# Seven block products for four in the first layer of the second FFN, with sums of weights made in the first FFN

## The chip, the cores and the metric

One core of a Trainium2 chip runs the whole program. The time is the device time of one execution in microseconds, and the kernel before ran three times: 799.74, 795.3 and 798.07, with a median of 798.07. The engines are TensorE (PE in the profile; its weight loads are PEld), VectorE (DVE), ScalarE (ACT), GpSimd (POOL) and SyncE (SP), which issues transfers only. All times below are in microseconds unless they are marked otherwise.

## The reference

The program is one "macaron" block over 8192 rows (8 x 1024) of H = 256 numbers in float32:

```python
x = x + 0.5 * ffn(x)          # first FFN   (x0 -> x1)
x = x + memory_layer(x)       # recurrent memory layer (x1 -> x2)
x = x + 0.5 * ffn(x)          # second FFN, the same weights (x2 -> out)

def ffn(x):                   # mixture of E = 8 experts, each row goes to its best one
    h = layernorm(x)
    p = softmax(h @ gate_w);  e = argmax(p)         # top 1
    # per expert the first CAP = 320 of its rows, in the order of the 8192
    y = relu(h[rows of e] @ w1[e]) @ w2[e]          # w1: 256 x 1024, w2: 1024 x 256
    return p[e] * y                                 # rows over the capacity get zero
```

The listing is a summary in the kernel's own terms. The layer norm's division is moved behind the ReLU: the kernel only subtracts the mean in front of the first layer, and the row's 1/std is part of the factor called `gate`.

## The kernel before

`macaron` (L1307) runs three stages one after the other: the first FFN (`first_router`, then `experts` with the name f1), `attention`, and the second FFN (`experts` with f2). x1 and x2 lie in DRAM. The router of the first FFN leaves the rows it has read in four SBUF tiles with the tag xt, and `copied` writes them to x1, so that rows which no expert takes stay as they are.

`experts` (L271) has a loop over the eight experts. Each expert takes 320 rows in three blocks of 128, 128 and 64 ("slots" s = 0, 1, 2). For expert e:

- `gather` (L284) brings the rows into xg by three indirect transfers on GpSimd's queue, two experts ahead; `gate_of` (L295) brings the factors into gate by three more.
- `center` (L306) subtracts each row's mean: statistics (L311), their aggregate (L312) and the subtraction (L313), all on VectorE.
- `turn` (L317) transposes the 320 rows on TensorE (L323) and copies the result to xT (L327, ScalarE). For expert 0 alone, `turn_one` (L330) does this block by block, and the first layer's matmuls begin with the first 128 rows.
- First layer: for each of the eight f (128 of the 1024 hidden features) two matmuls of 128 x 128 weights by 320 columns (L384), then a ReLU from PSUM to hT on ScalarE (L391).
- `turn` for expert e+1 follows, and then the second layer. First the last 64 rows are done, as two halves of 64 x 128 (16 matmuls, L414). VectorE multiplies by the gate and adds the row (L424) into xh, and xh is scattered to the result (L427). Then come the 128 rows of s = 0 and of s = 1 (8 matmuls each, L441), with VectorE's L448 into xo and a scatter (L451) for each.

The order of the instructions on each engine is the order in which the program writes them (`manual_schedule`). Each engine takes its own queue strictly in that order. GpSimd's queue holds, for an expert: two scatters of the expert before, three gates, the scatter of xh, three gathers, and so on. All scatters of a stage write the same DRAM tensor, and each waits until the one before it has landed.

The searches for which rows an expert takes (`Slots.begin`, `counts`, `tokens`) serve two experts at a time. A table `searches` puts them between the first layer's matmuls of experts 0, 1 and 2. They use TensorE for counting matmuls, ScalarE for a copy and VectorE for comparisons and sums.

`Weights.load` (L263) brings w1 and w2 of an expert, 1 MB each, on SP's queue; there are two buffers of each. The PSUM pool has the banks t (three), h (three) and y (two): t for the transposes, h for the first layer, y for the second.

The attention stage waits for the first FFN. Its first loads of x1 (L690, on ScalarE's queue) come behind all scatters. The list `ORDER` sets the order within that stage; it isn't changed. Its prologue prepares wg from w_g, b_g and norm_g (L601 to L605).

Of the kernel before, what the change touches and what calls it, by code (L numbers as in the profile page):

```python
# [10 lines left out]
F32 = mybir.dt.float32  # L11
# [7 lines left out]
P = 128  # L19
# [7 lines left out]
NS = 3  # L27
# [121 lines left out]
class Slots:  # L149
# [10 lines left out]
    def __init__(self, sh, pool, pp, dr, routed):  # L160
        self.sh, self.pool, self.pp, self.dr, self.routed = sh, pool, pp, dr, routed
# [25 lines left out]
    def spread(self, _):  # L187

        nc = self.sh.nc
        t_ps = self.pp.tile([P, 512], F32, tag="t", name="t_ps")  # L190
# [6 lines left out]
    def begin(self, q, between=lambda n: None):  # L197

        nc, sh, pool, pp = self.sh.nc, self.sh, self.pool, self.pp

        d_ps = pp.tile([P, 512], F32, tag="y", name="d_ps", bufs=2)
# [5 lines left out]
        between(1)  # L207
        b_ps = pp.tile([P, 512], F32, tag="h", name="b_ps")
        nc.tensor.matmul(b_ps[:, 0:1], lhsT=sh.before, rhs=dg[:, P - 1 : P], start=True, stop=True)
        between(1)  # L210
        began = pool.tile([P, NS * P], F32, tag="began", name="began", bufs=2)
        nc.vector.tensor_scalar(began, sh.jrow, b_ps[:, 0:1], None, ALU.is_ge)
        self.began = began

    def counts(self, q, tag="y"):
# [4 lines left out]
            self.pp.tile([P, 512], F32, tag=tag, name="r_ps", bufs={"y": 2, "h": 3}[tag])[  # L220
                :, : NS * (P + 1)
            ].rearrange("p (s r) -> p s r", s=NS)
# [34 lines left out]
class Weights:  # L257


    def __init__(self, nc, pool, w1, w2):  # L260
        self.nc, self.pool, self.w1, self.w2, self.at = nc, pool, w1, w2, {}

    def load(self, e):  # L263
        a = self.pool.tile([P, 2, F], F32, tag="w1", name="w1t")
        self.nc.sync.dma_start(a, self.w1[e].rearrange("(c p) f -> p c f", p=P))
        b = self.pool.tile([P, FC, H], F32, tag="w2", name="w2t")
        self.nc.sync.dma_start(b, self.w2[e].rearrange("(c p) d -> p c d", p=P))
        self.at[e] = a, b


def experts(sh, routed, src, dst, weights, dr, name, idle=0):  # L271
# [4 lines left out]
    nc, tc = sh.nc, sh.tc  # L276
    with ExitStack() as st:
        rp = st.enter_context(tc.tile_pool(name=f"{name}_r", bufs=1))
        ep = st.enter_context(tc.tile_pool(name=f"{name}_e", bufs=2))
        pp = st.enter_context(tc.tile_pool(name=f"{name}_p", bufs=3, space=PSUM))  # L280
        slots = Slots(sh, rp, pp, dr, routed)
# [24 lines left out]
        def center(xg):  # L306

            ln = ep.tile([P, NS, 8], F32, tag="ln", name="ln")
            xn = ep.tile([P, NS, H], F32, tag="xn", name="xn")
            for s in range(NS):  # L310
                nc.vector.bn_stats(ln[:, s, :6], xg[:, s, :])  # L311
                nc.vector.bn_aggr(ln[:, s, 6:], ln[:, s, :6])  # L312
                nc.vector.tensor_scalar(xn[:, s, :], xg[:, s, :], ln[:, s, 6:7], None, ALU.subtract)  # L313
            return xn

        def turn(xn):

            xT = ep.tile([P, 2, CAP], F32, tag="xT", name="xT")
            pts = [pp.tile([P, 512], F32, tag="t", name="pt") for _ in range(2)]
            for s in range(NS):  # L320
                m = min(P, CAP - s * P)
                for c in range(2):
                    nc.tensor.transpose(  # L323
                        pts[c][:, s * P : s * P + m], xn[:m, s, c * P : (c + 1) * P], sh.ident[:m, :m]
                    )
            for c in range(2):
                nc.scalar.copy(xT[:, c, :], pts[c][:, :CAP])  # L327
            return xT

        def turn_one(xn, xT, s):  # L330

            m = min(P, CAP - s * P)
            pt = pp.tile([P, 512], F32, tag="t", name="pt")
# [6 lines left out]
        def keep(n):  # L340

            if n:
                sh.idle(pp.tile([P, 512], F32, tag="y", name="idle", bufs=2), n)

        st.enter_context(tc.manual_schedule(engines=sh.engines))
        keep(idle)
        slots.begin(0, keep)
        slots.exps()
# [1029 lines left out]
```

## Time and profile before

| what | value |
|---|---|
| median of three runs | 798.07 |
| the profiled execution itself | 801.52 |
| its span in the profile | 799.7 |
| busy PE / VectorE / ScalarE / GpSimd | 731.1 / 454.4 / 348.0 / 473.6 |
| mean clock granted to TensorE | 0.968 |
| L384, first layer: matmuls, both FFNs | 147.3 in 576 records |
| L441, second layer: matmuls, both FFNs | 114.8 in 512 records |
| a steady expert slot of the first FFN (118.87 to 137.19) | 18.32 |
| from expert 1's slot to the last scatter (82.06 to 210.71) | 128.65 |
| first load of x1 in attention | 213.86 |
| start of the second FFN's first gate transfers | 638.85 |

The busy times are those of one execution, taken by the hardware profiler. A float32 matmul runs as two passes, and each pass is a record of its own, so one matmul of the program is two records. The records of neighbouring passes overlap[...]; the distance between the starts of two records is the price of a pass. A line of a timeline gives start, length, engine, line, operation, what it writes and reads, and in brackets the idle time before it and what released it.

### The profile page before, as it was taken

How to read it: one execution, taken by the hardware profiler on the slowest of the kernel's cores; microseconds unless marked ns; L12 is line 12 of the kernel's file. 1: busy time of each engine (PE TensorE's matmuls, PEld its weight loads, DVE VectorE, ACT ScalarE, POOL GpSimd, SP SyncE). 2: the span in 40 equal slices, each digit the busy share in tenths (PEclk: the TensorE clock that was granted, in tenths of full speed). 3: DMA queues.
4: the chain of work that ended last, by engine and by line, in shares of the span. 5: the costliest groups of instructions: out<-in, count | busy, mean ns of one | idle time of the engine just before them, and what ended most of it. 6: DMA issues, size and time to landing. Idle time of an engine off the chain costs nothing. (4 is left out here: it accounts for less than half of the span.)

```text
span 799.7 us, 13992 instructions
## 1 busy us (share of the span) xinstructions
PE 731.1 (91%) x5368; PEld 541.7 (68%) x5368; DVE 454.4 (57%) x941; ACT 348.0 (44%) x756; POOL 473.6 (59%) x606
## 2 busy tenths in 40 slices
PE   7988999999668999899999999999968789999997
PEld 5667777777425486666757576675755577778775
DVE  7772343220328978988887878888763624322310
ACT  5521222222057576767666666766443222222221
POOL 6643444552134788988888888886864434455431
PEclk9998999999968999999999989999999999999999
DMA  9995445540214242454454343444405814444510
GB/s 297 368 385 168 151 147 157 174 156 17 94 54 81 82 106 82 104 169 99 159 135 132 111 103 118 96 132 108 133 28 196 293 57 142 142 150 153 153 66 23
DMA packets 110946, 110.41 MB, mean 138 GB/s; under 512 B 12384, under 2 KB 103904, under 8 KB 110880
## 3 DMA queue, kind: packets, MB, share of 16 engines
q1 hardware_dynamic: 73152, 66.43, 28.0%
q10 hardware_dynamic: 31840, 31.53, 12.5%
q0 software_dynamic: 5888, 11.57, 4.7%
q8 instruction: 42, 0.69, 0.4%
q14 instruction: 24, 0.20, 0.1%
HBM read 78.80 MB, written 30.64 MB: 137 GB/s over the span
## 5 line engine op out<-in xcount | busy, mean ns | idle before, releaser
L391 ACT ACTIVATE hT<-ph 128x320 f32<-128x320 f32 (+2 forms) x144 | 58.3, 407 | 222.4 <-PE ph L384 196.4
L384 PE MATMUL ph<-xT,w1t 128*128 128x320 f32 (+2 forms) x576 | 147.3, 411 | 2.9 <-ACT hT L391 1.9
L384 PEld LDWEIGHTS ph<-xT,w1t 128*128 128x128 f32 x576 | 104.5, 194 | 37.7 <-ACT hT L391 2.2
L441 PE MATMUL py<-w2t,hT 128*128 128x256 f32 x512 | 114.8, 382 | 0.0
L441 PEld LDWEIGHTS py<-w2t,hT 128*128 128x128 f32 x512 | 96.0, 190 | 15.1 <-issue 2.7
L424 DVE SCALAR_TENSOR_TENSOR xh<-py,gate,xg 64x128 f32<-64x128 f32 x32 | 11.2, 350 | 111.5 <-PE py L414 111.2
L448 DVE SCALAR_TENSOR_TENSOR xo<-py,gate,xg 128x256 f32<-128x256 f32 x32 | 15.5, 484 | 94.3 <-PE py L441 59.2
L806 PE MATMUL pre<-xT,w 128*64 128x512 f32 x256 | 61.4, 603 | 0.8 <-ACT kk L838 0.8
L1142 PE MATMUL pre<-wg,xT 128*128 128x256 f32 x256 | 59.1, 390 | 2.0 <-DVE m L901 2.0
L298 POOL DMA_INDIRECT gate<-gate_d,get x48 | 46.0, 959 | 21.6 <-issue 13.4
L1142 PEld LDWEIGHTS pre<-wg,xT 128*128 128x128 f32 x256 | 49.0, 194 | 10.0 <-DVE m L901 2.4
L1186 POOL TENSOR_TENSOR xo<-xo,xr 128x512 f32<-128x512 f32 x32 | 42.9, 1354 | 17.4 <-DVE xo L1180 17.4
L708 ACT ACTIVATE xt<-xt,ln_nm,lx_t 128x256 f32<-128x256 f32 x64 | 34.4, 592 | 24.2 <-POOL ln_nm L703 24.2
L1180 DVE SCALAR_TENSOR_TENSOR xo<-tail,rs,gate 128x256 f32<-128x256 f32 x64 | 27.1, 475 | 23.7 <-DMA out<-xo 12.0
L427 POOL DMA_INDIRECT x<-xh,put x8 | 8.1, 1009 | 54.3 <-DVE xh L424 44.0
L995 DVE TENSOR_TENSOR gc<-ehd,c 128x1536 f32<-128x1536 f32 x16 | 40.0, 2539 | 0.3
L427 POOL DMA_INDIRECT out<-xh,put x8 | 8.1, 1013 | 52.5 <-DVE xh L424 52.5
L806 PEld LDWEIGHTS pre<-xT,w 128*64 128x64 f32 x256 | 15.8, 136 | 30.3 <-issue 22.4
L907 POOL TENSOR_TENSOR abq<-qq,ab 128x512 f32<-128x512 f32 x16 | 33.7, 2108 | 0.9 <-DMA ab<-kept 0.9
L715 PE MATMUL pre<-ident,xt 128*128 128x128 f32 x128 | 21.0, 298 | 14.3 <-ACT xt L708 12.9
L451 POOL DMA_INDIRECT out<-xo,put x16 | 16.1, 1006 | 27.5 <-DVE xn L313 14.2
L414 PE MATMUL py<-w2t,hT 128*64 128x128 f32 x512 | 32.2, 280 | 0.0
(259 smaller groups left out, 1612.5 us busy)
## 6 DMA issues: line engine op xcount, KB each, us to landing
w1t<-w_in SPq DMA_DIRECT2D x16, 1024.0 KB
w2t<-w_in SPq DMA_DIRECT2D x16, 1024.0 KB
xt<-hidden_in SPq DMA_DIRECT2D x16, 512.0 KB
x<-xt SPq DMA_DIRECT2D x16, 512.0 KB
xt<-x ACTq DMA_DIRECT2D x16, 512.0 KB
xr<-x ACTq DMA_DIRECT2D x16, 512.0 KB
x<-xo ACTq DMA_DIRECT2D x14, 512.0 KB
out<-xo ACTq DMA_DIRECT2D x14, 512.0 KB
```

The costliest lines, as they stand in the source:

```text
L298: nc.gpsimd.indirect_dma_start(out=gate[:, s : s + 1], out_offset=None, in_=slots.gate, in_offset=bass.IndirectOffsetOnAxis(ap=slots.get[: ...
L384: nc.tensor.matmul(ph[:, at_slots], lhsT=a[:, c, f * P : (f + 1) * P], rhs=at[:, c, at_slots], start=(c == 0), stop=(c == 1),)
L391: nc.scalar.activation(hT[:, f, at_slots], ph[:, at_slots], AF.Relu)
L414: nc.tensor.matmul(py[h * D : (h + 1) * D, :P], lhsT=hT[:, f, 2 * P :], rhs=b[:, f, h * P : (h + 1) * P], start=(f == 0), stop=(f == FC - ...
L441: nc.tensor.matmul(py[:, :H], lhsT=hT[:, f, s * P : (s + 1) * P], rhs=b[:, f, :], start=(f == 0), stop=(f == FC - 1),)
L708: self.nc.scalar.activation(x, x, AF.Identity, bias=u.nm[:, j : j + 1], scale=u.r16[:, j : j + 1])
L806: self.nc.tensor.matmul(ps[self.half[r], :], lhsT=self.w3[:, k, f * D : (f + 1) * D], rhs=u.xT[:, k].rearrange("h (p r t) -> h p r t", p=N ...
L907: self.nc.gpsimd.tensor_tensor(u.abq[:, n], u.kv[2], u.ab[:, n], ALU.mult)
L995: self.nc.vector.tensor_tensor(u.gc[:, layer], g.unsqueeze(2).to_broadcast([P, B, 3, D]), u.c3.rearrange("s n j -> s j n").unsqueeze(3).to ...
L1142: self.nc.tensor.matmul(ps[:, q * H : (q + 1) * H], lhsT=u.xT[:, k, j * P : (j + 1) * P], rhs=self.wg[:, k, :], start=(k == 0), stop=(k == 1),
L1180: self.nc.vector.scalar_tensor_tensor(u.xo[h][:, j, :], self.out_of(u, h, j), u.rs[h][:, j : j + 1], u.gate[n][:, j % 2, :], ALU.mult, ALU ...
L1186: self.nc.gpsimd.tensor_tensor(u.xo[h][:, two], u.xo[h][:, two], u.xr[h][:, two], ALU.add)
```

## The change

In the second FFN, from expert 1 on, the first layer is computed in another form. The 256 x 1024 weights are seen as four groups g of 256 x 256, each of them 2 x 2 blocks of 128 x 128, and xT as 2 x 2 blocks of 128 x 160. A product of 2 x 2 blocks is done with seven block products (Winograd's form) rather than eight. So a group has 7 matmuls of 128 x 128 weights by 160 columns, where it had 4 of 320 columns; the whole layer has 28 in place of 16. It needs four sums of weight blocks (s), four sums of blocks of xT (t, made by three VectorE operations in `row_sums`), and sums of the products, made by one ScalarE copy and VectorE operations on the way from PSUM to hT (`one` to `five`).

The sums of weights are 128 x 2048 numbers per expert. In the first FFN GpSimd makes them for experts 1 to 7 by four `tensor_tensor` operations of 128 x 512, and writes each expert's 1 MB to DRAM by a transfer on its own queue (`keep`). Both stand behind the gates of that expert. The second FFN loads them on SP's queue. In the first FFN the sums lie in the four buffers of the tag xt.

The further edits are these. The centered rows are negated: ScalarE computes mean minus row, the matmuls yield the negative, and ReLU has the scale -1. `center` for expert e+2 is issued in expert e's second layer, behind L424. `gate_of(e)` is issued at the start of expert e, where it was in expert e-1 at f = 1. `gather` runs three experts ahead. The searches stand in the second layer of experts 1 to 3; those of expert 0 stay in its first layer, with expert 2's gather and expert 1's `center` behind them at f = 1. The last 64 rows' second layer takes f = 6 last. PSUM has tags x, z, t and y, two banks each. In attention's prologue wg is computed by two operations of full size where it had two of full size and one small one.

```diff
+    def sums(self, e):
+        s = self.s[e] = self.place().rearrange("p a b -> p (a b)")[:, : 2 * F].rearrange(
+            "p (n g m) -> p n g m", n=4, m=P
+        )
+        if e in self.kept:
+            self.nc.sync.dma_start(s, self.kept[e])
+            return
+        (a11, a12), (a21, a22) = self.a[e]
+        for n, (x, y, op) in enumerate(
+            (
+                (a21, a22, ALU.add),
+                (s[:, 0], a11, ALU.subtract),
+                (a11, a21, ALU.subtract),
+                (a12, s[:, 1], ALU.subtract),
+            )
+        ):
+            self.nc.gpsimd.tensor_tensor(s[:, n], x, y, op)
+
+    def keep(self, e):
+        self.kept[e] = self.dr.tile([P, 4, FC // 2, P], F32, name=f"sums{e}")
+        self.nc.gpsimd.dma_start(self.kept[e], self.s[e])
...
         def center(xg):
-                nc.vector.tensor_scalar(xn[:, s, :], xg[:, s, :], ln[:, s, 6:7], None, ALU.subtract)
+                nc.scalar.activation(xn[:, s, :], xg[:, s, :], AF.Identity, bias=ln[:, 6:7], scale=-1.0)
...
+        def row_sums(xT):
+            nc.vector.tensor_tensor(t[:, 0:2], v[:, 1:4:2], v[:, 0:2], ALU.subtract)
+            nc.vector.tensor_tensor(t[:, 2], v[:, 3], t[:, 0], ALU.subtract)
+            nc.vector.tensor_tensor(t[:, 3], v[:, 2], t[:, 2], ALU.subtract)
...
             for f in range(FC):
                 hidden(f, slice(P if e == 0 else 0, CAP))
-                for search, n in searches.get((e, f), ()):
-                    search(n)
-                if f == 1 and e + 1 < E:
-                    gates.append(gate_of(e + 1))
+                if (e, f) == (0, 1):
+                    slots.counts(1)
+                    slots.tokens(2)
+                    rows.append(gather(2))
+                    xns[1] = center(rows[1])
+                if (e, f) == (0, 3):
+                    slots.tokens(3)
+                if (e, f) == (0, 5):
+                    slots.begin(2)
+                if (e, f) == (0, 6):
+                    slots.began_at()
...
+            def one(self, g):
+                x = self.x[g] = bank("x", "x")
+                self.product(x[:, :HC], self.s[:, 1], g, self.t[:, 2])
+                self.product(x[:, HC : 2 * HC], self.a[0][0], g, self.b[:, 0, 0], stop=False)
+                p6 = ep.tile([P, HC], F32, tag="p6", name="p6")
+                nc.scalar.copy(p6, x[:, :HC])
+                u = self.u[g] = ep.tile([P, HC], F32, tag="u", name="u", bufs=3)
+                nc.vector.tensor_tensor(u, x[:, HC : 2 * HC], p6, ALU.add)
+            def two(self, g):
+                z = self.z[g] = bank("z", "z")
+                self.product(z[:, :HC], self.s[:, 2], g, self.t[:, 1])
+                self.product(z[:, HC : 2 * HC], self.a[1][1], g, self.t[:, 3])
+                self.product(z[:, 2 * HC : 3 * HC], self.s[:, 0], g, self.t[:, 0], stop=False)
+                v = self.v[g] = ep.tile([P, 1, HC], F32, tag="v", name="v")
+                nc.vector.tensor_tensor(v[:, 0], z[:, :HC], self.u[g], ALU.add)
+            def three(self, g):
+                nc.vector.tensor_tensor(
+                    self.hT[:, 2 * g + 1, :].rearrange("p (j n) -> p j n", j=2),
+                    self.z[g][:, HC : 3 * HC].rearrange("p (j n) -> p j n", j=2),
+                    self.v[g].to_broadcast([P, 2, HC]),
+                    ALU.add,
+                )
+            def four(self, g):
+                x = self.x[g]
+                self.product(x[:, HC : 2 * HC], self.a[0][1], g, self.b[:, 1, 0], start=False)
+                nc.scalar.activation(self.hT[:, 2 * g, :HC], x[:, HC : 2 * HC], AF.Relu, scale=-1.0)
+            def five(self, g):
+                z = self.z[g]
+                self.product(z[:, 2 * HC : 3 * HC], self.s[:, 3], g, self.b[:, 1, 1], start=False)
+                nc.vector.tensor_tensor(self.hT[:, 2 * g, HC:], z[:, 2 * HC : 3 * HC], self.u[g], ALU.add)
+            def relu(self, f, a=0):
+                h = self.hT[:, f, a:]
+                nc.scalar.activation(h, h, AF.Relu, scale=-1.0)
...
+        searches = {
+            (1, 0): lambda: slots.counts(2),
+            (1, 1): lambda: slots.tokens(4),
+            (1, 2): lambda: slots.tokens(5),
+            (2, 0): lambda: slots.begin(3),
+            (2, 2): slots.began_at,
+            (3, 0): lambda: slots.counts(3),
+            (3, 1): lambda: slots.tokens(6),
+            (3, 2): lambda: slots.tokens(7),
+        }
         for e in range(E):
+            if 0 < e < E - 1:
+                if seven:
+                    weights.sums(e + 1)
+                weights.first(e + 1)
+                weights.second(e + 1)
+            if e > 0:
+                gates.append(gate_of(e))
+            if e > 0 and not seven:
+                weights.sums(e)
+                weights.keep(e)
+            if not seven or e == 0:
+                hT = plain(e, xn, xT)
+            else:
+                first = First(e, xT, t)
+                for g in range(G):
+                    first.one(g)
+                    if g > 0:
+                        first.four(g - 1)
+                    first.two(g)
+                    if g > 0:
+                        first.five(g - 1)
+                    first.three(g)
+                    if g > 0:
+                        first.relu(2 * g - 1)
+                        first.relu(2 * g - 2, HC)
+                first.four(G - 1)
+                first.relu(2 * G - 1)
             if e + 1 < E:
                 turn(xn[e + 1], xT)
+            if seven and e > 0:
+                first.five(G - 1)
+                first.relu(2 * G - 2, HC)
+            if seven and e + 1 < E:
+                t = row_sums(xT)
...
+            search(e, 0)
             for h in range(2):
                 part = slice(h * D, (h + 1) * D)
                 nc.vector.scalar_tensor_tensor(
                     xh[part], py[part, :P], gate[part, 2:3], xg[part, 2, h * P : (h + 1) * P], ALU.mult, ALU.add
                 )
+            if e + 2 < E:
+                xn[e + 2] = center(rows[e + 2])
+            search(e, 1)
             nc.gpsimd.indirect_dma_start(
...
-            if e + 2 < E:
-                rows.append(gather(e + 2))
+            if e + 3 < E:
+                rows.append(gather(e + 3))
             for s in range(2):
...
+                if s == 0:
+                    search(e, 2)
                 nc.gpsimd.indirect_dma_start(
```

## The prediction

> **What bounds the kernel now.** I read the engine totals first, then stretches of the trace, then GpSimd's timeline. "Expert slot" is the time in which TensorE works on one expert; S is its start.
>
> ```profile
> PE 731.1 (91%) x5368; PEld 541.7 (68%) x5368; DVE 454.4 (57%) x941; ACT 348.0 (44%) x756; POOL 473.6 (59%) x606
> ...
> 118.87:137.19 18.32, 18.32 (x103) 14.50 (x102) 4.43 (x13) 4.25 (x10) 8.77 (x10) 1.00 0.51 155
> 82.06:210.71 128.65, 127.11 (x718) 100.25 (x717) 33.04 (x99) 28.39 (x67) 51.82 (x53) 1.00 0.39 122
> ```
>
> The windows' columns are length, then busy time of PE, PE's weight loads, VectorE, ScalarE and GpSimd, then PE's clock, DMA share and GB/s. In a steady expert slot PE is busy for all 18.32 us; GpSimd shows 8.77. So PE sets FFN1's length, and a gain of PE in FFN2 counts in full. But GpSimd's busy time is not what its queue costs. Its timeline (start, length, what; in brackets the idle time before it and who ended it):
>
> ```profile
> 118.06 1.01 POOL L451 DMA_INDIRECT x<-xo,put  x1 [0.30 <-issue]
> 121.42 1.00 POOL L451 DMA_INDIRECT x<-xo,put  x1 [2.35 <-DVE ln L312]
> 122.72 0.98 POOL L298 DMA_INDIRECT gate<-gate_d,get  x1 [0.30 <-issue]
> ...
> 131.29 1.01 POOL L427 DMA_INDIRECT x<-xh,put  x1 [5.07 <-DVE xh L424]
> ...
> 207.26 0.98 POOL L451 DMA_INDIRECT x<-xo,put  x1 [2.43 <-DVE xo L448]
> 210.71 0.98 POOL L451 DMA_INDIRECT x<-xo,put  x1 [2.47 <-DVE xo L448]
> ```
>
> Each indirect transfer takes 1.0 and 0.3 follows before the next. Two scatters to x1 in a row stand 3.4 apart (118.06 to 121.42, 207.26 to 210.71): the second waits until the first has landed, since VectorE, named there, was done long before. In one slot this leaves 5.07 of true waiting for PE's result. That is all the room that GpSimd's queue has.
>
> **The change, 1: PE in FFN2.** Half-passes (every fp32 matmul is two) in fully busy stretches:
>
> ```profile
> 640.70:641.48 0.78, 0.78 (x8) 0.78 (x8) 0.43 (x2) 0.40 (x2) 0.48 (x2) 1.00 0.00 0
> 641.48:642.78 1.30, 1.30 (x10) 1.18 (x8) 0.00 (x0) 0.31 (x2) 0.99 (x2) 1.00 0.02 0
> 703.22:711.56 8.34, 8.34 (x32) 5.84 (x31) 3.25 (x10) 3.06 (x7) 3.89 (x4) 1.00 0.50 159
> ```
>
> These are 128, 192 and 320 moving columns, with other weights for each. Seven spacings in 0.78 are 0.112 (one record overlaps from before), eight in 1.30 are 0.1625, 31 in 8.34 are 0.269. Between 128 and 192 columns, 160 are an estimated 0.137. An expert's first layer goes from 16x2x0.269 = 8.61 to 28x2x0.137 = 7.67, so -0.94 for each of experts 1 to 7: -6.6.
>
> A rule speaks against it. The Trainium skill, "TensorE: Matmul & The Clock Gate", Part 3 (packing), has a weight load overlap a running matmul only where the row groups differ, and gives some 107 ns for 128 columns. Here all rows are used: 56x(0.133+0.107) = 13.4 per expert, +4.8 instead of -0.94, over seven +34. The rows decide: 0.112 at 128 columns holds no separate load. I take -6.6.
>
> What the block form adds beside PE: per group of two f's one ScalarE copy and three ReLUs (some 1.4 by L391's 0.28 to 0.41), and four VectorE sums (about 1.65 by L448's 0.48 and L424's 0.35), against 1.92 of PE. They hide; if a link is 0.5 later than PE can look ahead, it costs up to that in each of 28 groups (+14). The last product of a layer needs the last VectorE sum: six transposes (0.8) cover it in experts 1 to 6, for which I add 0.1 each, in expert 7 nothing does: +0.7. Searches leave the first layer: expert 1 takes 20.67 now, 2 takes 19.38; placed in the second layer I get 19.3, 19.2 and, for expert 3, 19.3 against 18.3: -0.4 together on PE's old base. The 1 MB more of loads on SP's queue per expert makes 3.7 MB in 17.4, or 215 GB/s, under the 385 of the page's early slices: nothing; without that cover 1 MB is 2.7. FFN2: -6.6+0.6+0.7-0.4 = -5.7.
>
> **2: GpSimd in FFN1.** Four sums and one 1 MB write per expert 1 to 7 now stand behind the gates and ahead of the scatter of xh, the gathers, and both scatters of xo, on the same queue. Price of one sum of 128x512:
>
> ```profile
> L1014 POOL TENSOR_TENSOR go<-go 128x512 f32<-128x512 f32 x7 | 9.1, 1294 | 0.6
> L907 POOL TENSOR_TENSOR abq<-qq,ab 128x512 f32<-128x512 f32 x16 | 33.7, 2108 | 0.9 <-DMA ab<-kept 0.9
> ```
>
> L1014 adds two strided halves, as the sums do: 1.29, and 0.06 to the next is 1.35. L907, beside a busy VectorE, takes 2.1. The skill's "GPSIMD Engine Reference", section 3.1, has some 2.6 cycles an element for two inputs, with 4497 ns for 2048; a quarter of that is an estimated 1.12, 28x0.23 = 6.4 less over the stage. The row decides, as it is this chip at this shape. The write (`keep`) has no row: nearest is an indirect transfer of 128 rows, 1.0+0.3; ends 0.4 (as ScalarE's queue pays at L195) and 2. I take 1.3.
>
> Period: gates 3x1.28 = 3.8, sums 5.4, keep 1.3, xh 1.3, gathers 3.8, first xo to second 3.4, to the next gate 1.3: 20.3, above PE's 18.3. So GpSimd sets FFN1's rate. Who waits: the gates of later experts come behind, so VectorE's line L424 (its place before the changed one), then the py bank, then PE, by a microsecond or two; no separate cost, since GpSimd stays last. Experts 1 to 4: 4x20.3, and 0.45 for expert 1's gather waiting for tokens(4): 81.7. Experts 5 and 6 have no gather; then the second scatter waits for xh's landing, 3.4, or 4.2 if behind the 1 MB: 3.8+5.4+1.3+3.8+3.4+1.3 = 19.0 each, 38.0. Expert 7 to its last scatter: the same without the last 1.3, 17.7. Sum 137.4 against 128.65 (82.06, first gate behind expert 0's scatters, to 210.71): +8.7. The attention stage waits 1:1 on that last scatter at 210.71:
>
> ```profile
> 213.59 0.52 POOL L631 MEMSET st<- 128x512 f32 x1 [1.90 <-PE pre L596]
> 213.86 1.52 ACTq L690 DMA_DIRECT2D xt<-x  x3
> ```
>
> The load of x1 is issued 2.15 after the last scatter's end. Bounds of the block: with sums of 1.05 (GpSimd's multiplications at L1010 take 1.06) and keep at 0.4, -14.7 of queue, of which PE's pace keeps all under 18.3: about +0.8. With sums of 2.1: 28x0.75 = +21 more.
>
> The subtraction in `center` goes from VectorE to ScalarE, both with room in steady slots: nothing (exposed 3x0.59, the mean of L708, per expert). The prologue's two lines for wg are hidden until x1 is loaded: nothing; exposed under 1.
>
> **3: expert 0, both FFNs.** Three Identity operations now stand in ScalarE's queue ahead of the first xT copy, and wait for the gather's third block:
>
> ```profile
> 50.30 0.37 ACT L336 COPY xT<-pt 128x256 f32<-128x256 f32 x1 [1.89 <-PE pt L335]
> ...
> 51.69 0.43 DVE L311 BATCH_NORM_STATS2 ln<-xg 128x6 f32<-128x256 f32 x1 [0.87 <-DMA xg<-hidden_in,get]
> ```
>
> The third statistics end at 52.3, and one Identity of 0.59 after 0.18 more leaves the copy at 53.1: +2.8 in FFN1, and by the same reckoning +1.8 in FFN2. Later, ScalarE's ReLU of f=1 stands behind center(1)'s Identities, which follow VectorE's tokens(2) (1.85 of small operations) and three statistics (0.61 each): 1.85+1.83+0.59 = 4.3, less some 2.4 for PE's two free banks and the count's matmuls: +1.9; and the new wait for `began` at f=6 +0.65. What may go away is this stretch as it is now:
>
> ```profile
> 59.00:63.27 4.27, 1.77 (x12) 1.43 (x10) 2.15 (x9) 0.66 (x3) 2.33 (x3) 1.00 0.86 290
> 63.27:70.10 6.83, 6.07 (x30) 5.53 (x32) 0.42 (x1) 2.12 (x7) 0.00 (x0) 0.50 0.22 58
> ```
>
> PE idles 3.3 (its b_ps comes late), then runs at half clock, losing 3.4; in FFN2 the like is 1.9 and 1.7. If both go, FFN1 changes by 2.8+2.55-3.3-3.4 = -1.35 and FFN2 by 1.8+2.55-1.9-1.7 = +0.75; if the half clock stays, +2.05 and +2.45; if the idling stays too, +5.35 and +4.35. An idle PE precedes the half clock here, and PE will idle for the 1.9 again, so I take values near the middle: +1.0 and +1.5.
>
> **Sum.** 8.7+1.0-5.7+1.5 = +5.5, on the profiled execution's 801.52 (span 799.7). The three runs had a median of 798.07, 3.45 less; the difference is carried over: 803.5.
>
> **Rivals.**
> A. GpSimd's cover holds (the other side). Place: its queue in FFN1; it decides where sums and keep fit in 18.3-13.6 = 4.7 a slot, for example sums at 0.95 and keep at 0.9. Then FFN1 gains only the tail, about +0.8, and with +0.8-5.7+2.5 it is 795.7; with expert 0 warm (-0.6 for 2.5) 792.6. For it: multiplications at 1.06, the skill's 1.12. Against: every addition at 128x512 takes 1.27 or more.
> B. GpSimd is slowed by VectorE, sums at 1.7 to 2.1: 28x0.35 to 0.75, so +10 to +21 more: 813 to 825. For it: L907; against: VectorE is 24% busy in the slot.
> C. The change doesn't do what it says on PE: ScalarE's or VectorE's chain bounds the first layer, and FFN2 gains nothing: 809. For it: 0.3 to 0.5 of room a group. With loads not overlapped, 840.
> D. The main case, but expert 0 at half clock and idle in both: 5.35+4.35 for 2.5, so 810.7.
>
> **How the numbers follow.** Main case with its own spread (799 to 811, D in it) 0.58; A 0.21, B 0.12, C 0.09. The range to 794 cuts off the lower half of A, to 815 most of B's. 0.5% is 4 us, about what a measurement of this kernel can tell from no change. Faster (under 794.1): half of A and a little, 0.13. Same (to 802.1): the rest of A and 0.15 of the main case, 0.26. Slower 0.61.
>
> **What would show it.** FFN1: GpSimd without true waiting in experts 1 to 4, slots of 20.3, PE idle in the later ones; x1 load about 10 later. FFN2: slots of 17.4 and half-passes at 0.137. The sums at 1.3 and keep at 1.3. It is wrong if the four sums end within 4.7 less keep, if the chain of `one` to `three` leaves gaps on PE, or if expert 0 goes the other way.

## The result and the profile after

The changed kernel takes 840.62 us (median of 4 runs, 837.91 to 846.82), the kernel before 798.78 (4 runs). The ratio is 1.0563, with a 95% interval of 1.0518 to 1.0609: slower by about 42 us. The prediction said 803.5, with a range from 794 to 815. The direction was right and the size was not.

The two profiled executions have spans of 799.7 and 840.8. The rows "first FFN" and "second FFN" of this table run between the issues of GpSimd's transfers, so they can be read off its timeline; "e0" is expert 0.

| stage | before | after | difference | predicted |
|---|---|---|---|---|
| to the second scatter of xo of e0, first FFN | 80.80 | 80.70 | -0.1 | +1.0 |
| first FFN, from there to its last scatter | 129.91 | 158.83 | +28.9 | +8.7 |
| attention: from there to the second FFN's first gather | 417.82 | 425.53 | +7.7 | 0 |
| second FFN, first gather to e0's second scatter of xo | 36.97 | 35.59 | -1.4 | +1.5 |
| second FFN, from there to its last scatter | 129.29 | 134.67 | +5.4 | -5.7 |
| behind the last scatter | 4.9 | 5.5 | +0.6 | 0 |

The engine totals and stretches that answer to those of before, from the page and from the windows view (length, busy time of PE, PE's weight loads, VectorE, ScalarE and GpSimd, PE's clock, DMA share, GB/s):

```profile
PE 740.4 (88%) x5536; PEld 562.7 (67%) x5536; DVE 483.1 (57%) x1025; ACT 378.7 (45%) x860; POOL 513.4 (61%) x641
```

```profile
82.01:239.53 157.52, 135.01 (x730) 104.60 (x729) 30.32 (x89) 35.49 (x81) 91.20 (x88) 0.95 0.42 142
...
736.94:744.28 7.34, 7.34 (x56) 7.34 (x55) 4.93 (x15) 3.41 (x12) 2.18 (x3) 1.00 0.64 203
744.41:765.30 20.89, 18.14 (x135) 16.02 (x134) 12.50 (x40) 6.75 (x21) 8.80 (x9) 1.00 0.57 186
```

PE is busy 9.3 longer than before and GpSimd 39.8. The first row of the windows is the first FFN from the first gate behind expert 0: 157.5 where it was 128.65, and PE now idles for 22 of it. TensorE's clock is 0.95 there, but that isn't what makes it longer. The scatter of xh, which needs TensorE's result, never waits on GpSimd's queue for more than the 0.3 that follow any instruction. Before, it waited 44.0 in all for VectorE's xh (GpSimd's waits over 80.7 to 210.8, with the total, the number of times and the longest):

```profile
POOL x L427 <- DVE xh L424: 44.0, 7, 9.8
```

The second row is the first layer of one expert of the second FFN in its new form. The 53 spacings of its 54 recorded half-passes are 0.135 to 0.137, so weight loads do not add to them. The third row is a slot of the second FFN: 20.89 long, of which PE is idle for 2.7.

Now GpSimd's timeline in the first FFN, one slot of the changed kernel from its gates to its second scatter of xo:

```profile
108.79 0.94 POOL L337 DMA_INDIRECT gate<-gate_d,get  x1 [0.30 <-issue]
109.76 1.29 POOL L293 TENSOR_TENSOR s<-w1t 128x512 f32<-128x512 f32 x1
...
113.58 1.28 POOL L293 TENSOR_TENSOR s<-w1t,s 128x512 f32<-128x512 f32 x1
115.15 0.60 POOL L297 DMA_DIRECT2D sums<-s  x1 [0.30 <-POOL s L293]
116.06 1.03 POOL L587 DMA_INDIRECT x<-xh,put  x1 [0.30 <-issue]
117.39 1.00 POOL L326 DMA_INDIRECT xg<-hidden_in,get  x1 [0.30 <-issue]
...
125.03 1.01 POOL L613 DMA_INDIRECT x<-xo,put  x1 [4.13 <-issue]
130.40 0.99 POOL L613 DMA_INDIRECT x<-xo,put  x1 [4.36 <-issue]
```

The four sums take 5.4 from 109.76 to the write at 115.15, as predicted. The write itself takes 0.9 of the queue, less than predicted. But the first scatter of xo goes out 9.0 behind that of xh, and the second 5.4 behind the first, where two scatters stood 3.4 apart before. These are waits for landings, 4.13 and 4.36, and the prediction had counted none for the first and some 2 for the second. The page's DMA list and SyncE's timeline of this slot show what travels at that time:

```profile
sums<-s POOLq DMA_DIRECT2D x7, 1024.0 KB, 8.7
```

```profile
114.88 0.37 SPq L266 DMA_DIRECT2D w1t<-w_in  x1
115.90 0.37 SPq L274 DMA_DIRECT2D w2t<-w_in  x1
```

w1's next load waits for a buffer that the sums read. It goes out when they end (114.88), w2's load stands behind it on SyncE's queue and follows (115.90), and the write comes between (115.15): 3 MB are issued in one microsecond, just ahead of the scatter of xh at 116.06. In the slots of experts 3 to 5 w1's load goes out 0.3 ahead of the write too, and w2's 2.3 to 2.9 behind it. The write needs 8.7 to land (median of seven).

The run holds a comparison of its own. Experts 5 and 6 both have sums and a write, and neither has a gather; but behind expert 5's sums the last loads of w1 and w2 go out (188.12 and 190.72), and behind expert 6's none does. From the scatter of xh to the first of xo it is 8.66 with the loads and 4.37 without:

```profile
189.28 1.02 POOL L587 DMA_INDIRECT x<-xh,put  x1 [0.30 <-issue]
197.94 0.99 POOL L613 DMA_INDIRECT x<-xo,put  x1 [7.63 <-issue]
...
212.20 1.02 POOL L587 DMA_INDIRECT x<-xh,put  x1 [0.30 <-issue]
216.57 0.99 POOL L613 DMA_INDIRECT x<-xo,put  x1 [3.36 <-DMA x<-xh,put]
```

VectorE had the rows for both ready (L608 ends at 187.5 and 208.5).

In the second FFN, VectorE's waits say which input of the first multiply by the gate (L424 before, L581 after) came last. The view's columns are the total, the number of times and the longest; before, over 660 to 770:

```profile
DVE xh L424 <- PE py L414: 40.4, 6, 7.7
```

After, over 690 to 810, and one of these in VectorE's timeline:

```profile
DVE xh L581 <- DMA gate<-gate_d,get: 22.7, 4, 5.8
```

```profile
732.61 0.71 DVE L581 SCALAR_TENSOR_TENSOR xh<-py,gate,xg 64x128 f32<-64x128 f32 x2 [5.82 <-DMA gate<-gate_d,get]
```

Before, it waited for PE. Now it waits for the gate, which GpSimd issued from 724.92 to 727.57, and TensorE waits for the bank that this multiply frees (its waits over 690 to 840):

```profile
PE py L601 <- DVE xh L581: 9.1, 4, 2.7
```

From expert 0's second scatter of xo to the last, PE is busy 128.1 of 129.3 before and 123.2 of 134.7 after. So the block products save what they should, and 10 of new idle time outweigh it.

### The profile page after: what moved, and what is told of

It reads as the page before. It is cut to its first block, busy times and chain, and to the rows that moved or that the text cites. A ratio compares the mean times of both kernels' runs of the same rounds, so it can differ in the third digit from the quotient of the medians.

```text
span 840.8 us, 14684 instructions
## 1 busy us (share of the span) xinstructions
PE 740.4 (88%) x5536; PEld 562.7 (67%) x5536; DVE 483.1 (57%) x1025; ACT 378.7 (45%) x860; POOL 513.4 (61%) x641
## 5 line engine op out<-in xcount | busy, mean ns | idle before, releaser
L601 PE MATMUL py<-w2t,hT 128*128 128x256 f32 x512 | 123.0, 397 | 26.0 <-DVE xh L581 26.0
L601 PEld LDWEIGHTS py<-w2t,hT 128*128 128x128 f32 x512 | 99.1, 198 | 45.3 <-DVE xh L581 29.6
L581 DVE SCALAR_TENSOR_TENSOR xh<-py,gate,xg 64x128 f32<-64x128 f32 x32 | 11.2, 350 | 140.0 <-DMA gate<-gate_d,get 124.3
L394 PE MATMUL ph<-xT,w1t 128*128 128x320 f32 (+2 forms) x352 | 83.4, 393 | 5.5 <-ACT xT L383 3.0
L394 PEld LDWEIGHTS ph<-xT,w1t 128*128 128x128 f32 x352 | 61.7, 196 | 23.7 <-ACT xT L383 3.5
L401 ACT ACTIVATE hT<-ph 128x320 f32<-128x320 f32 (+2 forms) x88 | 33.5, 388 | 79.4 <-PE ph L394 79.3
L352 ACT ACTIVATE xn<-xg,ln 128x256 f32<-128x256 f32 x48 | 24.3, 508 | 86.3 <-DVE ln L351 47.4
L1347 POOL TENSOR_TENSOR xo<-xo,xr 128x512 f32<-128x512 f32 x32 | 42.9, 1353 | 18.4 <-DVE xo L1341 18.3
L613 POOL DMA_INDIRECT x<-xo,put x16 | 16.0, 1000 | 53.9 <-issue 32.3
L608 DVE SCALAR_TENSOR_TENSOR xo<-py,gate,xg 128x256 f32<-128x256 f32 x32 | 15.5, 483 | 38.1 <-PE py L601 37.7
L326 POOL DMA_INDIRECT xg<-x,get x24 | 23.0, 960 | 19.1 <-issue 11.0
```

The costliest lines, as they stand in the source:

```text
L394: nc.tensor.matmul(ph[:, at_slots], lhsT=weights.w[e][:, c, f * P : (f + 1) * P], rhs=xT[:, c, at_slots], start=(c == 0), stop=(c == 1),)
L401: nc.scalar.activation(hT[:, f, at_slots], ph[:, at_slots], AF.Relu, scale=-1.0)
L601: nc.tensor.matmul(py[:, :H], lhsT=hT[:, f, s * P : (s + 1) * P], rhs=b[:, f, :], start=(f == 0), stop=(f == FC - 1),)
L613: nc.gpsimd.indirect_dma_start(out=dst, out_offset=bass.IndirectOffsetOnAxis(ap=slots.put[:, e, s : s + 1], axis=0), in_=xo[:, s, :], in_o ...
L1347: self.nc.gpsimd.tensor_tensor(u.xo[h][:, two], u.xo[h][:, two], u.xr[h][:, two], ALU.add)
```

## The experiments

"Stretch" is the second row of the first table, the first FFN from expert 0's second scatter of xo to the last scatter.

**Sums and write, each alone.** a1_no_write drops the write in `keep` (and loads w1 in place of the sums in the second FFN); a2_no_sums drops the additions and writes w1's tile; a3_write_on_sync changes the queue. Here and below, "..." stands for lines left out.

```diff
 a1:  -        self.nc.gpsimd.dma_start(self.kept[e], self.s[e])
      +        self.kept[e] = True
 ...
 a2:  -        for n, (x, y, op) in enumerate(
      +        for n, (x, y, op) in (lambda v: ())(
 ...
      -        self.nc.gpsimd.dma_start(self.kept[e], self.s[e])
      +        self.nc.gpsimd.dma_start(self.kept[e].rearrange("p n g m -> p (n g m)"), self.w[e].rearrange("p c f -> p (c f)"))
 a3:  -        self.nc.gpsimd.dma_start(self.kept[e], self.s[e])
      +        self.nc.sync.dma_start(self.kept[e], self.s[e])
```

> GpSimd makes the sums as in the changed kernel, but the 1 MB write per expert is left out; the second FFN loads the same number of bytes from w1 instead (so its first layers use wrong numbers). Measure: the first FFN from its first gate behind expert 0 to its last scatter, 128.7 us in the kernel before and 157.5 us in the changed one. Theory W (the write's packets, ahead of the scatters' in the same queue, hold up the landings on which the next scatter waits): experts 1 to 4 take 19.0 us, 5 and 6 fall back to 18.3, in all 130 to 133 us, so about 815 us of time. Theory Q (only the queue's instructions count, the write with 0.9): 157.5 less 7 x 0.9, 151 us, about 834 us.

> The four sums per expert are left out in the first FFN and the write takes w1's tile instead, 1 MB as well (the second FFN's first layers use wrong numbers). Theory W: the write still stands ahead of the scatters, but 5.4 us more lie between it and the scatter of xh, so most of it has landed: 130 to 137 us for the stretch. Theory Q: 157.5 less 7 x 5.4 is under TensorE's pace, so 129 us. A third theory, that the added traffic alone slows the loads and scatters: over 145 us.

> The write of the sums is issued on SyncE's queue, which carries the weight loads, in place of GpSimd's; all else as in the changed kernel. Theory W: the scatters have their queue for themselves, slots of about 19.2 us for experts 1 to 4 and 18.3 after, 131 to 135 us for the stretch, some 817 us of time. Theory Q: 157.5 less 7 x 0.9, 151 us. The theory of traffic as such: no better than 150 us, since the bytes and their time are the same.

| kernel | stretch | above before |
|---|---|---|
| before | 129.9 | |
| changed | 158.8 | +28.9 |
| a1, sums without the write | 137.8 | +7.9 |
| a2, write without the sums | 130.8 | +0.9 |
| a3, write on SyncE's queue | 149.6 | +19.7 |

The texts above count from the first gate, 1.3 later than this table; by their measure a1 has 136.5, a2 129.5 and a3 148.2. The sums alone cost 7.9, the write alone 0.9, and both 28.9. Part of this is slack: a little more work on GpSimd's queue hides where the queue waited for TensorE before. But the prediction had that slack in its sum and came to only 8.7 for both; the rest is in their meeting. a2 takes the meeting away as well as the sums. Its write reads w1's tile, so w1's next load waits for the write to land (SyncE's waits over 84 to 220):

```profile
SPq L266 <- DMA sums<-w1t: 66.2, 5, 17.4
```

So 0.9 is the price of a write that no load of w1 runs beside, not of a write as such. a2's 129.5 also lies as near to theory Q's 129 as to W's 130. Theory Q is out by a1 (151 expected). a1 ends somewhat over W's range; its w1 and w2 loads still go out together beside the scatter of xh (135.26 and 136.10, with the scatter at 135.4). a3 is a miss for W as it stood: with the scatters' queue free of the write, 19.7 of the 28.9 stay, close to what the theory of traffic as such expected. So it is not only that packets stand behind the write in one queue. In a3 the first scatter of xo still waits 3.88 for the landing of xh, and the second 3.68:

```profile
111.95 1.01 POOL L587 DMA_INDIRECT x<-xh,put  x1 [0.16 <-issue]
...
120.61 1.00 POOL L613 DMA_INDIRECT x<-xo,put  x1 [3.88 <-DMA x<-xh,put]
125.29 0.99 POOL L613 DMA_INDIRECT x<-xo,put  x1 [3.68 <-issue]
```

As whole executions, one each, the three took 818.2, 818.2 and 834.7, beside one of 808.1 of the kernel before. a2's stretch is 7.0 shorter than a1's, but its attention is 3.7 and its second FFN 2.9 longer. In the profiles with an unchanged second FFN (changed, a3, c1, c3, c4) this stage runs from 170.3 to 178.8 from the first gather to the last scatter; in the two longest (a3, c3) more than 10 of it are at half clock, in the changed kernel 3.4. So one such length is not good to better than some 8, and the stretches, not the whole times, carry the argument.

**When the 3 MB meet.** The next theory (B in the texts below) was that the sums release the loads at the wrong moment. c1_three_w1 was to take that away by a third buffer for w1. c3_write_later leaves the sums and moves the write to the next expert, on the same queue. c4_sums_ahead in addition makes the sums one expert ahead, so that they are not the last readers of the buffer that the next load needs.

```diff
 c1:  +        self.nw = 3 if place else 2
 ...
      -        a = self.pool.tile([P, 2, F], F32, tag="w1", name="w1t")
      +        a = self.pool.tile([P, 2, F], F32, tag="w1", name="w1t", bufs=self.nw)
 c3:  -                weights.sums(e)
      -                weights.keep(e)
      +            if e > 1 and not seven:
      +                weights.keep(e - 1)
      +            if e > 0 and not seven:
      +                weights.sums(e)
      +                if e == E - 1:
      +                    weights.keep(e)
 c4:  -                weights.sums(e)
 ...
      +            if e + 1 < E and not seven:
      +                weights.sums(e + 1)
```

> In the first FFN w1 has three buffers in place of two, so that its load for the next expert no longer waits for GpSimd's sums, which read the buffer; all else as in the changed kernel. Measure: from expert 0's second scatter of xo to the last one, 129.9 us in the kernel before, 158.8 us in the changed one, 137.8 us without the write, 149.6 us with the write on SyncE's queue. Theory B (burst: the sums release the w1 load, w2 follows, and with the write 3 MB are issued just ahead of the scatter of xh, whose landing the next scatter needs): only the write's 1 MB is left there, 137 to 143 us. Rival R (the scatters' packets queue behind the write's, whatever else runs): over 150 us.

> In the first FFN the write of an expert's sums is issued one expert later, still on GpSimd's queue, behind the next expert's gates and ahead of its sums; the same bytes, the same queue, the same sums. Then 5.2 us of sums lie between the write and the scatter of xh, and the write no longer meets the w1 and w2 loads that the sums release. Theory B (the meeting of 3 MB just ahead of the scatters): from expert 0's second scatter of xo to the last 138 to 143 us, close to the 137.8 us without any write. Rival (the bytes or the queue as such): over 152 us, close to the 158.8 us of the changed kernel.

> As c3 (the write one expert later than its sums, same queue), and GpSimd also makes the sums one expert ahead: sums(e + 1) behind the gates of expert e. So the w1 buffer that the next load needs is free when TensorE's first layer ends, not when the sums end. GpSimd's queue holds the same instructions as in c3 but for the last expert, which has no sums. Theory B (the sums release w1's and w2's loads together, 2 MB just as the scatter of xh is issued): from expert 0's second scatter to the last 131 to 138 us; c3 had 143.7 us, of which 5 us are the last expert's sums at most. Rival (GpSimd's instructions alone make the 13.8 us that c3 lies above the kernel before): 139 us or more.

c1 measured 158.0, and it doesn't decide between B and R. With three buffers SyncE ran one expert further ahead and waited for the sums again. Its load of w1 goes out 0.02 after a last sum ends (114.22 + 1.28), so the meeting was not taken away:

```profile
114.22 1.28 POOL L294 TENSOR_TENSOR s<-w1t,s 128x512 f32<-128x512 f32 x1
115.52 0.39 SPq L267 DMA_DIRECT2D w1t<-w_in  x1
116.23 0.37 SPq L275 DMA_DIRECT2D w2t<-w_in  x1
```

c3 measured 143.7, 0.7 above B's range and far from the rival's: the same bytes on the same queue, issued one expert later, take back 15.2 of the 28.9. The write now lands in 4.2 instead of 8.7. c4 measured 133.2, within B. Its sums for expert 1 stand in expert 0, whose second scatter comes at 84.12 instead of 80.98, so the ends are compared: the last scatter is at 217.3, against 224.7 in c3, 239.5 in the changed kernel and 210.7 before. Of the 10.5 between the stretches of c3 and c4, 5.9 are in the last expert's slot, which has no sums any more; the 4.6 in the slots of experts 1 to 5 are what keeping the loads apart is worth. In c4 the loads of w1 and w2 stand 8.6 to 14 apart again. Its longest remaining wait is where a load is issued just ahead of a scatter. Here w2's load goes out at 120.50:

```profile
121.58 1.02 POOL L614 DMA_INDIRECT x<-xo,put  x1 [0.30 <-issue]
128.10 0.99 POOL L614 DMA_INDIRECT x<-xo,put  x1 [5.50 <-issue]
```

**The second FFN's slots.** b1_gates_early issues the gates one expert earlier; c2_no_loads drops the 1 MB of sums from the loads.

```diff
 b1:  -            if e > 0:
      -                gates.append(gate_of(e))
      +            if e + 1 < E:
      +                gates.append(gate_of(e + 1))
 c2:  -            self.nc.sync.dma_start(s, self.kept[e])
 ...
      -                self.a, self.s = weights.a[e], weights.s[e]
      +                self.a = weights.a[e]
      +                self.s = weights.w[e].rearrange("p c f -> p (c f)").rearrange(
 ...
```

> gate_of(e + 1) is issued at the start of expert e, one expert earlier than in the changed kernel; all else as there. Theory G (in the second FFN the gates of an expert land too late for its first VectorE multiply, which holds a y bank that TensorE needs): its slots for experts 2 to 5 go from 20.0 to 20.9 us to 17.4 to 18.4, and from its first gather to its last scatter 156 us instead of 170.3 (166.3 before). Rival (the weights or the sums of weights come late): no change, 170 us. The first FFN stays within 3 us of 157.5, as GpSimd's queue holds the same work. Time about 827 us by G, 840 us by the rival.

> The second FFN loads no sums of weights; its block products take w1's tile in their place (so its first layers use wrong numbers), as many matmuls of the same shape. All else as in the changed kernel, the late gates too. Theory T (the added 1 MB, issued with w1's load at the moment of the gates, holds up their landing): slots of experts 2 to 5 fall from 20.0 to 20.9 us to some 18.5 us, and 157 to 161 us from the first gather to the last scatter instead of 170.3. Rival L (the gates are late by their place in the queue alone): slots stay over 20 us, 167 us or more.

| slot of expert (second scatter of xo to the next) | 1 | 2 | 3 | 4 | 5 | 6 | 7 |
|---|---|---|---|---|---|---|---|
| before | 20.68 | 19.37 | 18.30 | 18.28 | 18.35 | 18.37 | 15.93 |
| changed | 22.97 | 20.79 | 20.90 | 20.87 | 20.04 | 14.70 | 14.41 |
| b1 | 24.03 | 19.14 | 18.34 | 18.31 | 17.57 | 14.10 | 15.00 |
| c2 | 22.86 | 18.69 | 19.04 | 19.11 | 18.73 | 14.46 | 14.57 |

Either alone takes the 20.9 of experts 3 and 4 to 18.3 or 19.1, and TensorE's waits for L581 in the stage from 9.1 to 1.7 in c2 and none in b1. With an unchanged second FFN the slots of experts 2 to 4 are 20.3 to 22.5 in every profile (changed, a3, c1, c3, c4), so this is clear of their scatter. So the gates' place and the added load are both needed for the stall: the gates are issued when w1's load and the sums' are (723.93 and 725.10 in the changed kernel, the gates from 724.92). b1's slots came as theory G had them for experts 3 to 5, but the stage as a whole did not: it took 169.9 and not 156, as its expert 0 took 43.4 where the changed kernel took 35.6. b1's gates for expert 1 stand ahead of expert 2's gather there, which goes out 2.1 later. TensorE's clock also shows half speed for 10.2 us from 688.5 on. The first FFN stayed within the 3 that were expected. As a whole b1 took 842.4 and not theory G's 827 (one execution). c2 took 163.0 in all, between the two expectations but nearer to that of the added load.

**A version that takes both meetings away.** m1 does the changed kernel's arithmetic. m0 is m1 without the block products and all that serves them.

```diff
 m1:  -                gates.append(gate_of(e))
      +                gates.append(gate_of(e + 1))
      -                weights.sums(e)
      -                weights.keep(e)
      +                weights.sums(e, (2, 3))
 ...
      +                if e > 1 and f == 3:
      +                    weights.keep(e - 1)
 ...
      +                if s == 0 and e + 1 < E and not seven:
      +                    weights.sums(e + 1, (0, 1))
 ...
      -            self.nc.sync.dma_start(s, self.kept[e])
      +            self.nc.scalar.dma_start(s, self.kept[e])
 ...
      -        self.nc.gpsimd.dma_start(self.kept[e], self.s[e])
      +        self.nc.scalar.dma_start(self.kept[e], self.s[e])
```

> A version with the same arithmetic as the changed kernel, but gate_of runs one expert ahead again; the four sums of an expert are split, two between the two scatters of xo, where GpSimd waits for a landing anyway, and two behind the gates; the write goes out on ScalarE's queue one expert later, at f = 3, when no load runs; in the second FFN the sums are loaded by ScalarE's queue, those of expert 1 behind the gates' write and the others at g = 2, when no other load runs. Theories W and B together: the first FFN's stretch is 129 to 134 us (129.9 before, 158.8 in the changed kernel), the second FFN's from the first gather to the last scatter 158 to 163 us (166.3 before), so about 4 us under the kernel before, give or take 4 for the clock in the attention stage. Theory Q (GpSimd's queue is full, 17.6 of 18.3 us, and any wait shows): the first FFN over 140 us.

> The version m1 again, timed: the first look had 792.2 us beside 800.8 us. If its gain is real, the ratio to the kernel before is 0.985 to 0.995.

> m1 without the block products: four matmuls of 320 columns per group in the second FFN too, no sums, no writes and no loads of sums; the early gates, the moved searches and the other edits stay. If m1's gain is the block products' (0.94 us of TensorE for each of seven experts), m0 takes 5 to 7 us more than m1, about 798 us, ratio 0.995 to 1.0 to the kernel before; its second FFN takes 128 to 130 us from expert 0's second scatter to the last, where m1's takes 123.3. Rival (the gain is from the moves of searches and gathers alone): m0 within 2 us of m1.

| kernel | stretch, first FFN | second FFN, first gather to last scatter | median time | ratio to before |
|---|---|---|---|---|
| before | 129.9 | 166.3 | 797.39 (43 runs) | |
| m1, timed | 126.4 | 158.8 | 795.01 (22 runs) | 0.9969 (0.9946 to 0.9992) |
| m0 | 127.2 | 163.8 | 801.12 (22 runs) | 1.0047 (1.0025 to 1.0070) |

m1 is 0.3% faster than the kernel before, with an interval that ends just under 1, and 6.1 us faster than m0. That is the worth of the block products with all that serves them: the prediction had 6.6 less some losses of 1.3, and 5.0 of it show in the second FFN of the two profiles. The stretch of 126.4 is under the 129 to 134 that were expected. The ratio of 0.997 misses the 0.985 to 0.995 expected from the first execution (792.17), and single runs of m1 lie between 789.0 and 802.7. m0 is 3.7 slower than before, although both its FFNs are shorter in its profile. The two profiles can't settle this: m0's is of an execution 2.9 under its median, that of before 4.1 above its own. In m1 two of the sums fill the wait between the two scatters of xo:

```profile
135.03 1.00 POOL L620 DMA_INDIRECT x<-xo,put  x1 [1.19 <-DMA x<-xh,put]
136.05 1.29 POOL L296 TENSOR_TENSOR s<-w1t 128x512 f32<-128x512 f32 x1
137.42 1.27 POOL L296 TENSOR_TENSOR s<-s,w1t 128x512 f32<-128x512 f32 x1
140.66 1.01 POOL L620 DMA_INDIRECT x<-xo,put  x1 [1.97 <-DMA x<-xo,put]
```

One slot of its second FFN, 18.0 long, has PE busy throughout:

```profile
698.40:716.40 18.00, 18.00 (x137) 16.48 (x137) 12.89 (x40) 6.78 (x21) 8.93 (x9) 1.00 0.66 209
```

**Attention's 7.7 us.** The same instructions run in it; the windows view of the stage before and after:

```profile
225.80:628.50 402.70, 371.92 (x3287) 261.20 (x3287) 310.14 (x492) 253.62 (x531) 302.68 (x363) 0.96 0.42 116
```

```profile
254.90:665.00 410.10, 380.84 (x3287) 268.87 (x3287) 311.39 (x492) 253.97 (x532) 302.80 (x363) 0.94 0.41 114
```

GpSimd, VectorE and ScalarE are as busy as before; PE is busy 8.9 longer at a lower clock. The profiles list the stretches with half the clock, here counted from the stage's first matmuls: 28.6 us before, 51.3 after. Over all 13 profiles the stage's length goes with that sum, 408.5 + 0.33 for each us at half clock, with a correlation of 0.98; c4 has the most (68.1 us, 429.7). The 22.7 us more of half clock make 7.4 of the 7.7 by that line. So the 7.7 goes with the clock; no experiment set the clock and nothing else. What sets it isn't settled: c2 has the same slow first FFN (158.3) and a stage of 418.5 with 34.3 us at half clock.

## Why the prediction was wrong

**Right: TensorE's part.** The row of 0.112 at 128 columns was weighed against the Trainium skill's rule ("TensorE: Matmul & The Clock Gate", Part 3) that a weight load overlaps a running matmul only where the row groups differ. The half-pass of 160 columns was predicted at 0.137 and measured 0.136; the estimate by the rule was 0.240. The rule was quoted without the exception that the same part makes for a background weight buffer, and its 107 ns follow from a formula in Part 2 of the page ("LDWEIGHTS (loading the stationary operand)"). The gain of the block products is 6.1 us where they can show (m0 against m1).

**Right: GpSimd becomes the bound of the first FFN, and the prices of its instructions.** The sums were put at 1.35 apiece, 5.4 together, and took 5.4. One takes 1.26 to 1.29, so the 1.12 estimated from the Trainium skill's figure ("GPSIMD Engine Reference", section 3.1) was too low for this shape. The write took 0.9 and not 1.3. The sums alone, without the write, cost 7.9 in the stretch, where the whole block was put at 8.7. That they come so close is in part luck: a1's slots run from 23.1 down to 16.3, where 20.3 to 17.7 were predicted with the write.

**Wrong: the landing waits in GpSimd's period.** The step that failed is the period's "xh 1.3, gathers 3.8, first xo to second 3.4": it has no wait at all between xh and the first xo, which the gathers were to hide, and 3.4 between the two of xo. Both came from a trace in which no load goes out just ahead of a scatter. Before, w1's load was issued 8.8 into a slot, 3.6 ahead of the scatter of xh, and w2's 9.7 later, 1.0 behind a scatter of xo. After, the sums hold w1's buffer, and w1, the write and w2 leave together around the scatter of xh. Over the seven experts the time from xh to the first xo is 20.9 more than was counted (8.7 to 9.1 for experts 1 to 5, where 5.1 was counted with gathers and 3.8 without; 4.4 for experts 6 and 7, where it was 3.8), and that between the two of xo 4.3 more. The rest of the period, from there to the next xh, is 4.9 less, by the cheaper write and shorter steps. This makes the 20.2 by which the stretch is longer than predicted, of the 35.6 that were missed in all (41.1 measured between the spans, 5.5 predicted). a1, a2, c3 and c4 show it: each one that takes one of the partners away or moves it in time takes half of the 28.9 back or more. The numbers above don't say which of the partners holds up a scatter by how much.

**Wrong: "nothing" for the 1 MB more of loads in the second FFN.** It compared 215 GB/s with the 385 that the chip had shown. That is a mean over a slot, and what counts is when the load is issued. The added load goes out with w1's while the gates are fetched. m1 loads the same bytes later in the slot and fetches the gates earlier, and TensorE has no wait for this multiply in its second FFN. **Wrong: no price for the gates' place there.** The prediction said for the first FFN who waits behind the late gates (L424, then the y bank, then TensorE), but charged nothing, since GpSimd would be the last anyway; in the second FFN, where it isn't, the same chain was not costed. In the changed kernel it stalls TensorE by 2 to 3 in a slot. With -5.7 predicted and +5.4 measured, the two terms are 11 us of the miss, of which TensorE's waits for L581 make 9.1.

**Wrong by size: expert 0.** +1.0 and +1.5 were predicted, -0.1 and -1.4 measured. The first gates of the second FFN come 13.3 behind its first gather instead of 10.3, with 2 MB more of loads on the way when their write goes out; in m1, which issues these loads later, they come at 10.3. That cost nothing that shows, as m1's expert 0 is as long there (35.5 and 35.6). Which term was too large isn't known; of the half clock, 3.4 of 6.8 stayed in the first FFN, and all 3.4 in the second.

**Not in the sum at all: attention, +7.7.** The prediction moved the stage as a whole with the last scatter and put its own length at no change without giving a reason. The length went with the clock, and why the clock was lower stays open.

Of the rivals none was it: A and B asked about the price of a sum, and that was right as taken. C's branch "with loads not overlapped, 840" has the measured time by chance: with half-passes of 0.136 no separate load is there, and by the prediction's own +34 that branch would give some 844. The range's upper end came from B, so it held no case in which a transfer lands later than in the trace of before.

## What to carry to other kernels

When a step reads a buffer that a load is waiting for, it sets when that load goes out, and with it all loads behind it on that queue; write down what else is on its way at that moment, not only the mean rate. A wait for a landing that is read off a quiet stretch is a lower bound for a stretch with loads in it. Two parts that cost 7.9 and 0.9 when kept apart cost 28.9 together here, so transfers that are on their way at one time are to be costed together, and idle time in front of a landing is the place for other work.

## What the runs showed of the hardware

- After a scatter of 128 rows of 1 KB the next one, which waits for its landing, goes out 3.4 behind it where no load was just issued, and also where a 1 MB load is issued 1.0 behind it (136.38 to 139.74 before, with w2's load at 137.38). It goes out 6.4 to 7.3 behind it where such a load was issued 0.8 to 1.6 ahead (four times in a2, once in c4), and 4.2 to 4.8 where that was 3.3 to 4.1 ahead (c4 and a2).
- A 1 MB write from SBUF to DRAM took 8.7 to land beside 2 MB of loads issued within some 3 us of it (median in the changed kernel), and 4.2 and 5.7 when it was issued apart from them (c3 and c4). It costs GpSimd's queue 0.6 and the 0.3 behind it.
- Moving a write to another queue does not keep it from delaying the transfers of the first: 19.7 of 28.9 us stayed in a3.
- Sums of 128x512 on GpSimd with strided inputs took 1.26 to 1.31 in the changed kernel, c3 and c4, also while VectorE worked.
- The time that the attention stage spends at half clock ran from 28.6 to 68.1 us over the kernels here, with the same instructions, and the stage was longer by 0.33 us for each.
